# Row scaling of the second layer on VectorE in two halves, and a new order of work inside a step of a two-layer graph attention kernel

## The chip, the cores and the metric

The kernel runs on one core of one Trainium2 chip. The metric is the device time of one execution in microseconds. The core's engines run their own instruction streams and meet through semaphores: TensorE (PE, with weight loads shown as PEld), VectorE (DVE), ScalarE (ACT), GpSimd (POOL) and SyncE (SP).

## The reference

A graph of N = 6250 nodes and E = 200000 edges, sorted by destination, goes through a layer norm, a ReLU and two graph attention (GAT) layers with 256 features, the first with 4 heads, the second with 1. Each edge has 32 attributes. Cut to what matters, one layer is:

```
te  = relu(edge_attr @ We + be) * exp(x @ Wo + bo)[src][:, None]   # 64 per edge
# self loops are added; their attribute is the mean of a node's incoming te
hx  = x @ Wg                                   # 256 per node
he  = te @ Wge                                 # enters the logits through a_e
al  = leaky_relu((hx . a_s)[src] + (hx . a_d)[dst] + he . a_e, 0.2)
m   = segment_max(al, dst)
al  = exp(al - m[dst]);  al = al / segment_sum(al, dst)[dst]
out = segment_sum(hx[src] * al[:, :, None], dst) + b
```

The first layer ends in relu(out + x), the second in out + x; the input is added at the end. Everything is float32.

## The kernel before, in words

**Tiling.** The sorted edges are cut into chunks of 128 and superchunks of C = 24 chunks (3072 edges). A layer has 66 superchunks; each is one *step*, described by a dictionary `st`. The loop `edges` (line 788) runs over the 132 steps of both layers. In the iteration of step `st` the next step `nx` is prepared. The last three steps of each layer are handled by `ending` (line 885), so 63 iterations of each layer take the regular path.

**What a step does**, with the function, the line and the engine:

- `gather` (L1065, POOL): 24 indirect DMAs fetch the rows `hx[src]` and a few columns beside them from a table in HBM, one row per partition and one chunk per DMA, into the tile G (128 x 24 x 270). There are three G buffers. A gather into a buffer waits until the sums of the step that used it before have ended. POOL does hardly anything else, so it runs ahead of the other engines.
- `spread` (L1189, L1190, DVE, once for two steps): builds one-hot tiles of the edges' places within their step, `lb` and Q. `parts` (L1296 to L1299, DVE, once for two steps; L1304, PE) splits the destination logits of the nodes into three bfloat16 parts and brings them into the layout wanted. `blocks` (L1311, DVE) copies them into a block form `aq`. `adst` (L1318, 2 matmuls) adds the destination's part to the logits of the edges.
- `rphase1` (L1165, PE; L1166, ACT): relu of the edge attributes times We, in pieces; `rphase2` (L1174, 8 matmuls): their product with the folded a_e. Both, and `adst`, end in one PSUM tile `zad`.
- `edge_rows` (L1332, L1335, DVE): turns `zad` into logits per edge. `logits` (L1346 to L1363, DVE) adds the source part and runs segmented maximum scans. `ends` (L1370, PE), `links` (L1380, L1382, DVE; L1387, PE) and `maxima` (L1397 to L1423, DVE, with the exp L1419 on ACT) carry the maxima across the partitions' borders and yield the weights exp(al - m). `ends` and `links` use the PSUM tile `lf`.
- scaling: G's rows are multiplied by the weights. In layer 0 `scale` does this for all 24 chunks in one VectorE instruction (L1454, 128 x 6144). In layer 1 `scale_rows` does it in 24 instructions of ScalarE (L1463, 128 x 256 each).
- `carried` (L1436 to L1444, DVE): adds the sum carried over from the step before to G's first row.
- `sums` (L1473, PE): per chunk one float32 product of a one-hot tile S (edge to destination) with G, added up in the PSUM tile `u`. In the trace one chunk is two weight loads and two matmuls, so a step has 48 of each.
- `onehots` (L1280, L1283, DVE): S for the next step. `evict` (L1478, ACT): `u` to SBUF. `finish` and `rows1` to `rows3`: the softmax's division, self loops, node update and, in layer 0, the table rows of layer 1.

**The order** is written out by hand: each engine executes in the order in which the loop body issues. Before the change it is: gather(nx), logits, ends, spread(nx), parts(nx), first piece of rphase1(nx), links, rows2, blocks(nx), maxima, the other pieces of rphase1(nx), rphase2(nx), adst(nx), scaling, carried, sums, rows3, onehots(nx), finish of the step before, evict, rows1, edge_rows(nx). The SP queue only issues loads and stores (`nodes` ahead of the gather, `load_lb`, `load_fl` after rows2, `load_ea` after rphase1) and the DMA instructions of `rows3`.

The one place that chooses between the engines is `st["rows"] = st["L"].l`: it is 0 in layer 0 and 1 in layer 1, and `maxima` and the loop test it.

Of the kernel before, what the change touches and what calls it, by code (L numbers as in the profile page):

```python
# [22 lines left out]
F32 = mybir.dt.float32  # L23
# [8 lines left out]
P = 128  # L32
C = 24
# [48 lines left out]
class Kernel:  # L82
# [705 lines left out]
    def edges(self, ctx):  # L788
        nc = self.nc
        steps = self.steps  # L790
        if self.NS % 2:
            self.load_lb(1)
        pv = late = None
        self.ahead, self.rest = 1, None
        for k, st in enumerate(steps):
            nx = steps[k + 1] if k + 1 < len(steps) else None
            if st["s"] + 2 >= self.NS:
                continue
            for q in steps[k + 1:k + 3]:
                if q["L"] is st["L"] and "tw" not in q:  # L800
                    self.nodes(q)
            self.load_lb(k + 2)
            left = 99
            if self.ahead < len(self.groups):
                left = self.groups[self.ahead][0] - 2 - (self.ahead + 2 >= len(self.groups)) - k
            if self.rest is None and left <= 2:
                gi = self.index_load(self.ahead, self.xp)
                self.rest = self.index_group(self.ahead, self.xp, gi)
            if st["L"].l and (st["s"] == 2 or st["s"] + 3 == self.NS) and not hasattr(self, "flag_i"):
                self.flag()  # L810
                if self.early:
                    self.window()
            if st["s"] + 3 == self.NS:
                self.ending(st, *steps[k + 1:k + 3], pv, late, steps[k + 3] if k + 3 < len(steps) else None)
                pv = late = None
                continue
            if 3 <= k + 1 < 6 and nx["L"].l == 0:
                nx["own"] = steps[k - 2]["G"]
            if k:
                self.gather(nx)  # L820
                st["rows"] = st["L"].l
                drain(self.logits(st))
                self.ends(st)
            self.spread(nx)
            self.parts(nx)
            y = self.rphase1(nx)
            next(y)
            if k:
                self.links(st)
            if late:  # L830
                self.rows2(late)
            self.load_fl(k + 1)
            self.blocks(nx)
            if k:
                drain(self.maxima(st))
            drain(y)
            self.load_ea(k + 2)
            self.rphase2(nx)
            self.adst(nx)
            if "S" not in st:  # L840
                self.onehots(st)
            if k:
                if st["rows"]:
                    self.scale_rows(st)
                else:
                    drain(self.scale(st))
                self.carried(st)
                self.sums(st)
            if late:
                self.rows3(late)  # L850
                late = None
            self.onehots(nx)
            if pv:
                drain(self.finish(pv))
            self.evict(st)
            if pv:
                self.rows1(pv)
                late = pv
            self.index_on(left)
            if k == 4 and self.early:  # L860
# [287 lines left out]
    def rphase1(self, st):  # L1148
# [11 lines left out]
        for a, b in self.pieces(c):  # L1160
# [5 lines left out]
            nc.scalar.activation(R[:, :, w], y[:, :, :n], AF.Relu, bias=self.be[l])  # L1166
            yield

    def rphase2(self, st):

        nc, l, R = self.nc, st["L"].l, st["R"]
        for w, o in self.halves(st):
            for i in range(2):
                nc.tensor.matmul(st["zad"][i * PH:(i + 1) * PH, o], self.wea[l][0], R[:, i, w],  # L1174
                                 start=True, stop=False)
# [107 lines left out]
            nc.vector.tensor_tensor(st["S"][:, c0:c1, :], self.k_iota.unsqueeze(1).to_broadcast(w),  # L1283
                                    self.loc[:, o + c0:o + c1].unsqueeze(2).to_broadcast(w), op=OP.is_equal)

    def parts(self, st):

        L, V = st["L"], self.nc.vector
        H = L.H
        if "a3" not in st:  # L1290
            q = [q for q in self.steps[st["k"]:st["k"] + 2 - st["k"] % 2] if q["L"] is L and "tw" in q]
            n, i = len(q), st["k"] % 4
            ad = self.tw4[:, i:i + n, L.ad:L.ad + H]
            a3 = self.wp.tile([P, 2, 4, 3], BF, name="a3")
            r = self.wp.tile([P, 2, 4], F32, name="a3r")
            V.tensor_copy(a3[:, :n, :H, 0], ad)  # L1296
            V.tensor_sub(r[:, :n, :H], ad, a3[:, :n, :H, 0])
            V.tensor_copy(a3[:, :n, :H, 1], r[:, :n, :H])
            V.tensor_sub(a3[:, :n, :H, 2], r[:, :n, :H], a3[:, :n, :H, 1])  # L1299
            for j, t in enumerate(q):  # L1300
                t["a3"] = a3[:, j]
        a3 = st["a3"]
        st["zad"] = z = self.ps_1.tile([P, 1024], F32, name="zad")
        self.nc.tensor.matmul(z[:, 400:400 + 3 * H], st["Q"], a3[:, :H, :].rearrange("p h t -> p (h t)"),  # L1304
                              start=True, stop=True)
# [159 lines left out]
    def sums(self, st, *parts):  # L1465
        nc, L, c = self.nc, st["L"], st["C"]
        G, S = st["G"], st["S"]
        for a, b in parts or ((0, c),):
            for i in range(a, b):
                j = st["n"] = st.get("n", -1) + 1  # L1470
                if j == 0 and "u" not in st:
                    st["u"] = self.ps_1.tile([P, 512], F32, name="u")
                nc.tensor.matmul(st["u"][:, :L.W], S[:, i, :], G[:, i, 0:L.W], start=(j == 0), stop=(j == c - 1))  # L1473
# [282 lines left out]
def drain(g):  # L1756
    for _ in g:
        pass
# [85 lines left out]
```

## Time and profile before

| | |
|---|---|
| median of 3 runs | 4928.91 us (4916.35 to 4935.57) |
| profiled execution | 4925.46 us |
| its span, first to last instruction | 4923.7 us |
| mean granted TensorE clock | 0.725 |
| regular steps of layer 0 | about 220 to 2374 us |
| regular steps of layer 1 | about 2608 to 4838 us |

The regular steps of the two layers make up 4384 of 4924 us. Within each layer the 63 steps are alike, so a step's time, times 63, is what a change is worth there. In the profile's lines a group shows its instructions (after x), their busy time, the mean of one and the engine's idle time before them with what ended most of it; "issue" means that the engine waited for nothing that the profile shows, and "remote" that the releaser is not known.

### The profile page before, as it was taken

To read this page: it belongs to the slowest core of one execution; us is meant where nothing else is said; L and a number is where in the kernel's file an instruction comes from. 1 tells how busy PE (TensorE), PEld (TensorE's weight loads), DVE (VectorE), ACT (ScalarE), POOL (GpSimd) and SP (SyncE) were. 2 spreads that over 40 slices of the span, in tenths; PEclk is the share of its full clock that TensorE was granted. 3 is DMA by queue.
4 is the path that set the end of the run, shared out by engine and by line. 5 is a ranking of instruction groups with operands and counts; after the bars stand their busy time and mean duration, and the time that the engine had idled before them with its cause. 6 is when DMAs were issued, how large, how long until landed. Compare 5 with 4: busy or idle time off the path is not lost.

```text
span 4923.7 us, 38114 instructions
## 1 busy us (share of the span) xinstructions
PE 2940.4 (60%) x10100; PEld 1841.8 (37%) x10100; DVE 2462.7 (50%) x6148; ACT 1132.2 (23%) x2701; POOL 2989.0 (61%) x3216
## 2 busy tenths in 40 slices
PE   6655666666666666665646556555565555655656
PEld 5433433343333434343434333333333333333334
DVE  5556666676666666666734323333333332333335
ACT  4211111111111111111103323233233332323322
POOL 6356666666666666666544656656666666666663
PEclk8777777777777777777777667667667676666767
DMA  7144444444444444444433434434444443443442
GB/s 223 55 119 125 126 128 134 123 135 132 133 124 128 135 126 131 129 135 122 122 109 92 121 106 115 122 105 119 114 118 114 112 121 107 116 118 107 118 117 71
DMA packets 248253, 591.97 MB, mean 120 GB/s; under 512 B 65849, under 2 KB 105125, under 8 KB 247783
## 3 DMA queue, kind: packets, MB, share of 16 engines
q0 software_dynamic: 150048, 422.51, 32.7%
q1 hardware_dynamic: 97009, 164.82, 10.5%
q10 hardware_dynamic: 976, 2.12, 0.2%
q8 instruction: 86, 1.41, 0.1%
q14 instruction: 134, 1.10, 0.1%
HBM read 544.23 MB, written 45.36 MB: 120 GB/s over the span
## 4 chain that ended last, share of the span: by engine, by line
issue 29%; PE 28%; DVE 21%; POOL 13%; another core or an unknown queue 5%; DMA 3%; ACT 1%; SPq 0%; DVEq 0%; ACTq 0%; POOLq 0%
PE u L1473 21%; POOL G L1065 12%; DVE G L1454 7%; DMA G<-T,src 3%; PE y L1165 2%; DVE S L1283 2%; PE zad L1174 2%; DVE m L1402 1%; DVE lb L1189 1%; DVE rt L1332 1%; ACT R L1166 1%; DVE t1rows L1638 1%; DVE fb L1397 0%; PE lf L1370 0%
## 5 line engine op out<-in xcount | busy, mean ns | idle before, releaser
L1065 POOL DMA_INDIRECT G<-T,src x3066 | 2912.9, 950 | 1824.8 <-issue 949.2
L1473 PE MATMUL u<-G,S 128*128 128x270 f32 (+1 forms) x6212 | 1873.3, 448 | 1419.9 <-issue 1202.2
L1473 PEld LDWEIGHTS u<-G,S 128*128 128x128 f32 x6212 | 1355.8, 221 | 1871.8 <-issue 1438.5
L1463 ACT ACTIVATE G<-G,kw 128x256 f32<-128x256 f32 x1512 | 609.0, 496 | 0.0
L1380 DVE TENSOR_TENSOR_SCAN cl<-fl,cl,lf 4x129 f32<-4x129 f32 (+1 forms) x130 | 61.1, 470 | 1007.6 <-PE zad L1304 940.1
L1478 ACT ACTIVATE U<-u 128x270 f32<-128x270 f32 (+1 forms) x130 | 51.0, 393 | 2169.3 <-PE u L1473 1686.5
L1454 DVE TENSOR_TENSOR G<-G,kps 128x6144 f32<-128x6144 f32 (+6 forms) x86 | 441.7, 5150 | 0.0
L1283 DVE TENSOR_TENSOR S<-kps,loc 128x3072 f32<-128x3072 f32 (+1 forms) x135 | 438.1, 3245 | 4.7
L1165 PE MATMUL y<-ea,webd 64*128 64x256 f32 (+2 forms) x1056 | 355.0, 762 | 41.0 <-ACT R L1166 35.3
L1174 PE MATMUL zad<-R,wea 128*64 128x384 f32 (+1 forms) x1056 | 285.0, 677 | 156.6 <-issue 87.5
L1166 ACT ACTIVATE R<-y,webd 128x1024 f32<-128x1024 f32 (+3 forms) x264 | 235.4, 892 | 427.5 <-PE y L1165 161.9
L1174 PEld LDWEIGHTS zad<-R,wea 128*64 128x64 f32 x1056 | 82.9, 177 | 395.8 <-issue 263.4
L1505 DVE SCALAR_TENSOR_TENSOR mg<-U,mw 128x1 f32<-128x1 f32 x65 | 14.4, 221 | 364.1 <-remote 170.6
L1165 PEld LDWEIGHTS y<-ea,webd 64*128 64x128 f32 x1056 | 116.0, 269 | 105.6 <-issue 59.3
L1332 DVE STREAM_TRANSPOSE rt<-zad 128x768 f32<-128x768 f32 (+1 forms) x130 | 125.8, 968 | 5.4 <-remote 5.4
L567 PE MATMUL fin<-wg,h1T 128*128 128x260 f32 x264 | 116.8, 587 | 1.5 <-ACT h1T L1565 1.5
L1189 DVE TENSOR_TENSOR lb<-lb,kps 128x1536 bf16<-128x1536 bf16 (+1 forms) x68 | 112.9, 1661 | 0.0
L1436 DVE SCALAR_TENSOR_TENSOR G<-U,kw,G 1x257 f32<-1x257 f32 x62 | 29.5, 476 | 152.4 <-issue 87.0
L1575 ACT ACTIVATE t1rows<-t1rows 128x1 f32<-128x1 f32 x66 | 13.4, 203 | 363.9 <-DVE t1rows L571 147.4
L1370 PE MATMUL lf<-ident,fb 128*36 128x128 f32 (+1 forms) x132 | 52.0, 394 | 55.8 <-DVE fb L1363 45.6
L1318 PE MATMUL zad<-lb,aq 128*128 128x384 bf16 (+2 forms) x264 | 83.8, 409 | 0.0
L1515 ACT ACTIVATE mw<-mw 128x8 f32<-128x8 f32 x66 | 13.8, 209 | 298.7 <-issue 146.9
(275 smaller groups left out, 2366.7 us busy)
## 6 DMA issues: line engine op xcount, KB each, us to landing
ea<-in_ea_dram SPq DMA_DIRECT2D x64, 768.0 KB
G<-T,src POOLq DMA_INDIRECT x3066
lb<-locrow SPq DMA_DIRECT2D x64, 384.0 KB
nd<-t1rows SPq DMA_DIRECT2D x66, 225.8 KB
tw<-nd SPq DMA_DIRECT2D x66, 225.8 KB
tw<-T SPq DMA_DIRECT2D x66, 117.2 KB
T<-t1rows SPq DMA_DIRECT2D x66, 113.8 KB
tw<-in_x_dram SPq DMA_DIRECT2D x66, 112.0 KB
```

The source lines that it names most:

```text
L567: self.nc.tensor.matmul(ps[:, :L.MW], hT[:, k, :], self.wg[L.l][:, k, :], start=(k == 0), stop=(k == 1))
L1065: nc.gpsimd.indirect_dma_start(out=G[:, c, 0:L.TW], out_offset=None, in_=st.get("from", self.T[L.l])[0:self.N, :], in_offset=bass.Indirect ...
L1165: nc.tensor.matmul(y[:, i, :n], self.webd[l][r, :], ea[r, w], start=True, stop=True)
L1166: nc.scalar.activation(R[:, :, w], y[:, :, :n], AF.Relu, bias=self.be[l])
L1174: nc.tensor.matmul(st["zad"][i * PH:(i + 1) * PH, o], self.wea[l][0], R[:, i, w], start=True, stop=False)
L1189: V.tensor_tensor(lb[:, :, :n], lb[:, :, :n], self.k_part.unsqueeze(2).to_broadcast([P, i, n]), op=OP.is_equal)
L1283: nc.vector.tensor_tensor(st["S"][:, c0:c1, :], self.k_iota.unsqueeze(1).to_broadcast(w), self.loc[:, o + c0:o + c1].unsqueeze(2).to_broad ...
L1318: self.nc.tensor.matmul(st["zad"][:, o], st["aq"].rearrange("p k j -> p (k j)"), st["lb"][:, w], start=False, stop=True)
L1332: V.transpose(rv[:, :32 * c].rearrange("p (b n) -> p b n", b=2), z.rearrange("p (b n) -> p b n", b=2)[:, :, :16 * c])
L1454: nc.vector.tensor_tensor(v, v, pw[:, c0:c1, :].unsqueeze(3) .to_broadcast([P, c1 - c0, H, L.F]), op=OP.mult)
L1463: self.nc.scalar.activation(v, v, AF.Copy, scale=st["w"][:, c:c + 1])
L1473: nc.tensor.matmul(st["u"][:, :L.W], S[:, i, :], G[:, i, 0:L.W], start=(j == 0), stop=(j == c - 1))
```

## The change

`st["rows"]` is set to 0 in both layers, so that layer 1 takes VectorE's `scale` as well; `scale_rows` and a third order for it remain in the text but are not reached. `scale` now runs in two halves of 12 chunks, with `carried` between them. In every iteration but the first the order is: gather(nx), logits, ends, first piece of rphase1(nx), links, rows2, maxima, the other pieces of rphase1(nx), rphase2(nx), first half of scale, carried, second half, spread(nx), sums of chunks 0 to 13, parts(nx), blocks(nx), sums 14 to 18, adst(nx), sums 19 to 23, rows3, onehots(nx), and then as before. `parts` writes its result no longer into columns 400 on of `zad` but, when given a bank, into columns 240 on of the tile `lf`; `zad` is then allocated by `rphase2` through a new helper. In the first iteration the old order stays, with adst and onehots of the next step moved behind each other. `ending` calls `parts` as before.

```diff
             if k:
                 self.gather(nx)
-                st["rows"] = st["L"].l
+                st["rows"] = 0
                 drain(self.logits(st))
                 self.ends(st)
-            self.spread(nx)
-            self.parts(nx)
+            else:
+                self.spread(nx)
+                self.parts(nx)
             y = self.rphase1(nx)
             next(y)
             if k:
@@
             self.load_fl(k + 1)
-            self.blocks(nx)
             if k:
                 drain(self.maxima(st))
-            drain(y)
-            self.load_ea(k + 2)
-            self.rphase2(nx)
-            self.adst(nx)
+            else:
+                self.blocks(nx)
+            if k and st["rows"]:
+                self.scale_rows(st)
+                drain(y)
+                self.load_ea(k + 2)
+            else:
+                drain(y)
+                self.load_ea(k + 2)
+                self.rphase2(nx)
             if "S" not in st:
                 self.onehots(st)
-            if k:
-                if st["rows"]:
-                    self.scale_rows(st)
-                else:
-                    drain(self.scale(st))
+            if not k:
+                self.adst(nx)
+                self.onehots(nx)
+            elif st["rows"]:
...
+            else:
+                f = self.scale(st, cuts=(0, C // 2, C))
+                next(f)
+                self.carried(st)
+                drain(f)
+                self.spread(nx)
+                self.sums(st, (0, 14))
+                self.parts(nx, self.lf)
+                self.blocks(nx)
+                self.sums(st, (14, 19))
+                self.adst(nx)
+                self.sums(st, (19, C))
+                if late:
+                    self.rows3(late)
+                    late = None
+                self.onehots(nx)
             if late:
                 self.rows3(late)
                 late = None
-            self.onehots(nx)
             if pv:
                 drain(self.finish(pv))
             self.evict(st)
@@
+    def zad(self, st):
+
+        if "zad" not in st:
+            st["zad"] = self.ps_1.tile([P, 1024], F32, name="zad")
+
     def rphase2(self, st):
 
+        self.zad(st)
@@
-    def parts(self, st):
+    def parts(self, st, bank=None):
@@
-        st["zad"] = z = self.ps_1.tile([P, 1024], F32, name="zad")
-        self.nc.tensor.matmul(z[:, 400:400 + 3 * H], st["Q"], a3[:, :H, :].rearrange("p h t -> p (h t)"),
+        if bank is None:
+            self.zad(st)
+        st["ad"] = z = st["zad"][:, 400:400 + 3 * H] if bank is None else bank[:, 240:240 + 3 * H]
+        self.nc.tensor.matmul(z, st["Q"], a3[:, :H, :].rearrange("p h t -> p (h t)"),
                               start=True, stop=True)
@@
     def blocks(self, st):
-                                     st["zad"][:, 400:400 + 3 * H].unsqueeze(1).to_broadcast([P, 4, 3 * H]),
+                                     st["ad"].unsqueeze(1).to_broadcast([P, 4, 3 * H]),
```

More of the change, by code (lines that the diff above doesn't have):

```diff
@@ L832, in edges @@
             self.load_fl(k + 1)
-            self.blocks(nx)
             if k:
                 drain(self.maxima(st))
-            drain(y)
-            self.load_ea(k + 2)
-            self.rphase2(nx)
-            self.adst(nx)
+            else:
[8 more added lines that the diff above has]
+                self.rphase2(nx)
             if "S" not in st:
                 self.onehots(st)
-            if k:
-                if st["rows"]:
-                    self.scale_rows(st)
-                else:
-                    drain(self.scale(st))
-                self.carried(st)
-                self.sums(st)
+            if not k:
+                self.adst(nx)
+                self.onehots(nx)
+            elif st["rows"]:
+                self.carried(st)
+                self.sums(st, (0, C // 3))
+                self.spread(nx)
+                self.parts(nx, self.lf)
+                self.sums(st, (C // 3, C))
+                self.rphase2(nx)
+                self.onehots(nx)
[6 more added lines that the diff above has]
+                drain(f)
+                self.spread(nx)
+                self.sums(st, (0, 14))
+                self.parts(nx, self.lf)
+                self.blocks(nx)
+                self.sums(st, (14, 19))
+                self.adst(nx)
+                self.sums(st, (19, C))
+                if late:
+                    self.rows3(late)
+                    late = None
+                self.onehots(nx)
             if late:
```

## The prediction

> **What bounds the kernel now.** I read the page first: engine shares, the chain, the costliest lines.
>
> ```profile
> PE 2940.4 (60%) x10100; PEld 1841.8 (37%) x10100; DVE 2462.7 (50%) x6148; ACT 1132.2 (23%) x2701; POOL 2989.0 (61%) x3216
> ...
> issue 29%; PE 28%; DVE 21%; POOL 13%; another core or an unknown queue 5%; DMA 3%; ACT 1%; SPq 0%; DVEq 0%; ACTq 0%; POOLq 0%
> ...
> L1065 POOL DMA_INDIRECT G<-T,src x3066 | 2912.9, 950 | 1824.8 <-issue 949.2
> L1473 PE MATMUL u<-G,S 128*128 128x270 f32 (+1 forms) x6212 | 1873.3, 448 | 1419.9 <-issue 1202.2
> ...
> L1463 ACT ACTIVATE G<-G,kw 128x256 f32<-128x256 f32 x1512 | 609.0, 496 | 0.0
> ```
>
> No engine is busy more than 61% of the span, and the largest share of the chain is "issue", time without a recorded cause. POOL is the regular part: one gather takes 0.95 us and the next follows 0.30 us later, so the 24 gathers of a step take 24 x 1.25 = 30 us. What POOL waits for between two such streams is in the waits, cut to the 63 regular steps of each layer: first layer 0, then layer 1.
>
> ```profile
> POOL G L1065 <- PE fin L1563: 217.1, 35, 25.0
> POOL G L1065 <- PE u L1473: 143.3, 28, 9.2
> ```
> ```profile
> POOL G L1065 <- PE zad L1304: 376.5, 58, 8.3
> ```
>
> The rows name what PE did last at that moment; the binding event is the end of the sums (L1473), since a gather writes the buffer that those sums read. Layer 1 waits 376.5/58 = 6.5 us a step. Layer 0, without one long wait of 25.0, (217.1 - 25.0 + 143.3)/62 = 5.4 us. So a step is 30 us of gathers and the stretch until the sums of the oldest buffer have ended. Why they end late is seen in the timeline of one step of layer 1 (start, length, engine, line; in brackets the idle time before it).
>
> ```profile
> 3497.76 0.94 POOL L1065 DMA_INDIRECT G<-T,src  x1 [7.00 <-PE zad L1304]
> ...
> 3500.22 0.25 DVE L1423 COPY G<-kw 128x24 f32<-128x24 f32 x1 [0.18 <-ACT kw L1419]
> ...
> 3502.84 9.67 ACT L1463 ACTIVATE G<-G,kw 128x256 f32<-128x256 f32 x24
> ...
> 3502.99 2.83 PE L1174 MATMUL zad<-R,wea 128*64 128x384 f32 x8 [1.22 <-issue]
> 3503.37 0.48 DVE L1436 SCALAR_TENSOR_TENSOR G<-U,kw,G 1x257 f32<-1x257 f32 x1 [2.90 <-issue]
> ...
> 3503.77 0.20 DVE L1444 SCALAR_TENSOR_TENSOR G<-U,slink,G 1x2 f32<-1x2 f32 x1
> ...
> 3505.76 0.82 PE L1318 MATMUL zad<-lb,aq 128*128 128x384 bf16 x2
> ...
> 3506.37 8.86 PE L1473 MATMUL u<-G,S 128*128 128x261 f32 x37
> ...
> 3517.62 0.52 PE L1473 MATMUL u<-G,S 128*128 128x261 f32 x1 [2.39 <-issue]
> ...
> 3519.03 0.29 PEld L1473 LDWEIGHTS u<-G,S 128*128 128x128 f32 x1 [3.31 <-issue]
> ...
> 3526.59 0.95 POOL L1065 DMA_INDIRECT G<-T,src  x1 [0.30 <-issue]
> ...
> 3531.03 3.05 PE L1473 MATMUL u<-G,S 128*128 128x261 f32 x6 [2.21 <-issue]
> ...
> 3534.11 0.39 ACT L1478 ACTIVATE U<-u 128x261 f32<-128x261 f32 x1 [21.41 <-PE u L1473]
> ...
> 3534.35 0.94 POOL L1065 DMA_INDIRECT G<-T,src  x1 [6.81 <-PE zad L1304]
> ```
>
> The sums begin 8.6 us into the step, and 37 of 48 pass in 8.86 us (0.24 us each). Then a matmul and the next weight load stand 1.4 us apart (3517.62, 3519.03), 2.8 us a pair, with "issue" before each. Only some 4 us after the last gather's start the remaining ones run together again. ScalarE's row scaling (9.67 us, ended at 3512.51) is not what the late sums wait for. Something limits how many instructions pass while POOL streams. The windows count them (busy time and, after x, instructions): from POOL's restart to the first stall, in two steps of layer 1 (rows 1 and 2) and two of layer 0 (rows 4 and 5), and inside a stall (row 3).
>
> ```profile
> core 0: us, PE busy (x) PEld busy (x) DVE busy (x) ACT busy (x) POOL busy (x), PEclk, DMA share, GB/s
> 3461.00:3479.00 18.00, 15.18 (x56) 9.40 (x57) 8.41 (x23) 11.92 (x29) 13.73 (x15) 0.75 0.50 148
> 3497.70:3515.50 17.80, 15.62 (x57) 9.55 (x56) 8.21 (x22) 11.99 (x29) 13.48 (x15) 0.72 0.37 98
> 3515.50:3531.00 15.50, 2.90 (x5) 1.62 (x6) 2.70 (x9) 0.00 (x0) 9.29 (x10) 0.57 0.52 135
> 1478.30:1504.60 26.30, 20.53 (x71) 13.92 (x72) 18.80 (x38) 4.26 (x10) 18.95 (x21) 0.77 0.58 166
> 1514.00:1540.50 26.50, 18.04 (x62) 11.20 (x62) 22.23 (x48) 4.12 (x10) 20.33 (x21) 0.74 0.45 119
> 2607.00:2620.00 13.00, 12.92 (x56) 10.42 (x54) 6.00 (x15) 6.26 (x16) 8.78 (x10) 0.89 0.31 83
> 2620.00:2639.00 19.00, 0.00 (x0) 0.00 (x0) 0.00 (x0) 0.00 (x0) 12.97 (x14) 0.59 0.37 98
> 2639.00:2662.00 23.00, 17.37 (x65) 11.40 (x65) 10.60 (x32) 12.56 (x30) 1.89 (x2) 0.74 0.11 32
> ```
>
> Layer 1 reaches 56+57+23+29+15 = 180 and 57+56+22+29+15 = 179 instructions after 18.0 and 17.8 us; layer 0 reaches 212 and 203 after 26.3 and 26.5. Row by row that is one budget that grows with time, (207 - 180)/(26.4 - 17.9) = 3.2 a us: an estimate from four rows. In the stall, 5 matmuls and 6 weight loads pass in 15.5 us.
>
> The last three rows, from layer 1's first step, tell what follows when the sums do end in time. All 48 ended inside the stream; then in 19 us every engine but POOL executed nothing (x0) while POOL issued 14 gathers, and only after that the engines ran a whole step in 22 us. The timeline of that place:
>
> ```profile
> 2639.62 0.39 ACT L1478 ACTIVATE U<-u 128x261 f32<-128x261 f32 x1 [26.36 <-remote]
> ...
> 2649.24 11.47 PE L1473 MATMUL u<-G,S 128*128 128x261 f32 x48
> ...
> 2660.99 0.94 POOL L1065 DMA_INDIRECT G<-T,src  x1 [20.18 <-PE fin L1049]
> ```
>
> **The change, part by part.** *Row scaling of layer 1.* 24 instructions of ScalarE (496 ns each, L1463) go, and with them PE's wait for each row. VectorE gets two halves; a whole one is in the rows of layer 0:
>
> ```profile
> 1514.08 0.94 POOL L1065 DMA_INDIRECT G<-T,src  x1 [4.82 <-PE u L1473]
> ...
> 1515.70 1.73 DVE L1189 TENSOR_TENSOR lb<-lb,kps 128x1536 bf16<-128x1536 bf16 x1
> ...
> 1517.35 0.42 DVE L1190 TENSOR_TENSOR Q<-kps,qsel 128x256 bf16<-128x256 f32 x1
> 1517.68 0.17 DVE L1296 CAST a<-tw 128x8 bf16<-128x8 f32 x1
> ...
> 1522.20 6.54 DVE L1454 TENSOR_TENSOR G<-G,kps 128x6144 f32<-128x6144 f32 x1
> 1522.98 0.95 POOL L1065 DMA_INDIRECT G<-T,src  x1 [0.30 <-issue]
> ```
>
> So 6.54/2 = 3.3 us a half. The maxima end at 3500.47, 2.7 us into the step; half one ends at 6.0, the carried row (0.48 + 0.20, less a little overlap) at 6.7, half two at 10.0. PE cannot begin sums before its own L1174 group ends (3505.82, 8.1 us), where now 0.8 us of L1318 follows. The sums thus begin at 8.1 instead of 8.6 us: by durations alone the gain is 0.5 us. The half-two wait is covered, since the first 12 chunks are 24 matmuls, 5.8 us at 0.24.
>
> *Spreading, parting, blocks* (1.73 us in every second step, four small casts, one product) leave the head of the step and run on VectorE beside the sums. In layer 0 they stand ahead of the links: in the step above the spreading held VectorE from 1515.70. PE's L1304 and L1318 now stand inside the sums behind chunks 14 and 19. What queues behind them are the last ten and five chunks. VectorE's part is ready at about 10.0 + 1.73 + 0.42 + 0.7 = 12.9 us (1517.35 and 1517.68, the other three casts taken as the first), before PE reaches chunk 14 at 8.1 + 28 x 0.24 = 14.8 us, so I cost them at nothing; without that cover they would cost the 1 to 2 us of a round trip. No DMA is added. SP's loads keep their order, and POOL's gathers still stand first in its queue; what moves is when their wait is met.
>
> *The instruction budget in layer 1.* This decides. From restart to the end of the sums PE issues 69 matmuls (48 + 8 + 8 + 2 + 1 + 1 + 1) and 69 loads; VectorE, counted by the code's order, about 28; ScalarE 5 instead of 29; POOL 15: 186. At 20 us (8.1 + 48 x 0.24 + 0.8 for the two moved groups = 20.4) the budget is 180 + 3.2 x 2.3 = 187. Before, the same end asked for about 22 more, and the sums fell into the stall with 11 to go. After, they end free of it or with a few pairs in it. Up to three pairs at 2.8 us bring the end to 28 us, still inside the 30 us stream. So I take it that POOL finds its buffer free and streams on without a wait.
>
> *What the next stream then does.* The budget is used up and POOL does not pause; I take the freeze of the three windows. Of 60 us of gathers the engines get about the first 20, and after the second stream POOL waits for a whole step: 20.2 us there (the bracket at 2660.99). Per two steps that replaces 2 x 6.5 = 13.0 us: +7.2, that is +3.6 a step, 63 x 3.6 = +227 us. Bounds: the one long wait of layer 0, 25.0 us, gives (25.0 - 13.0)/2 x 63 = +378; if the engines creep on and only 48 sums are left at the end, 11.5 us (the row at 2649.24), it is (11.5 - 13.0)/2 x 63 = -47. I take 20.2, since it is from layer 1 and from the same kind of step.
>
> *Layer 0.* The sums start earlier in the steps with spreading, at about 9 us, but need 150 of PE, some 40 of VectorE, 8 of ScalarE and 17 of POOL = 215 at 22 us, where the budget is 207 - 3.2 x 4.4 = 193. Some ten pairs stay in the stall, so POOL keeps its wait, at the least seen there. That least is about 4.8 us (the restart at 1514.08 had 4.82 before it): 62 x (5.4 - 4.8) = 37, taken as -40. Bounds: -90 if the late steps all become as the early ones; +378 if the sums escape here, too.
>
> *The rest* (the prologue, the two endings, where little but the order of layer 1's scaling changes) I put at 0, between -10 and +10: three of 66 steps a layer, at most about 3 us each.
>
> Sum, against the profiled execution (4925.46 us, span 4923.7): 4925.5 + 227 - 40 = 5112; the median of the runs shown is 3.4 us above that execution, so 5115.
>
> [...] While L1454 reads two operands (1522.20 to 1528.74) a gather takes 0.95 us (1522.98), which is the mean of all 3066. [...]
>
> **Rivals.** *A, faster: the stall still catches the sums of layer 1.* The point is seven or eight instructions: with four or more pairs left at the stall, 4 x 2.8 us carries the end from 20 past 30 us, and POOL waits again. For it: my 186 and 187 are equal within what I can count. Then layer 1 takes layer 0's least, 4.8 instead of 6.5: 63 x 1.7 = -107, with layer 0's -40: 4925.5 - 147 + 3.4 = 4782.
> *B, no freeze.* POOL never waits in layer 1 and the engines keep up: 63 x 6.5 = -410, -40: 4479. Against it: a step has over 200 instructions, and 30 us at 3.2 pass about 96.
> *C, no change.* The stall ends a fixed time behind the last gather whatever was done before, and the tail of pairs, evictions and restart stays 6.5 us; layer 0's 40 us shrink to under 25: about 4915.
> *D, gathers slowed by VectorE.* Half a scaling, 3.3 us, is lost by POOL in each layer-1 step: 63 x 3.3 = +208, less 40: 5097. The gathers of layer 0 speak against it.
>
> **How the numbers follow.** My forecast has 0.55, A 0.27, B 0.05, C 0.08, D 0.02, and 0.03 goes to layer 0 leaving its waits as well (5112 + 378, about 5490). The forecast's own range is 4925.5 - 47 - 90 = 4790 to 4925.5 + 378 - 10 = 5295, most of it above 5000; less the ends, 4980 to 5270. With A's 4782 the range over both signs is 4765 to 5270. Half a per cent, 25 us, is about what the three runs (4916 to 4936) can tell from no change. Faster: A, B and the low end of the forecast, 0.27 + 0.05 + 0.05 = 0.37. Same: C, 0.08. Slower: 0.50 of the forecast, D and the last, 0.55.
>
> **What would show it.** Right: in layer 1 POOL's waits fall to half their number, each near 20 us; windows in which every engine but POOL has x0; evictions (L1478) idle in pairs, one short and one over 20 us; L1473's "issue" idle falls. L1463 shrinks to the last steps of the layer or goes, and L1454 gets two instructions a step in layer 1. In layer 0 the waits stay at 63, near 4.8. Wrong: POOL's waits in layer 1 keep their number (A or C by their length), gathers over 0.95 us beside L1454 (D), or steps of 30 us without waits (B). The weakest step is the count of 186 against 187.

## The result: 8.8% slower, and the profile after

The changed kernel takes 5363.01 us (median of 4 runs, 5357.17 to 5363.5) against 4927.24 us before: ratio 1.0883, 95% interval 1.086 to 1.0906. The forecast was slower, 5115 us, with a range up to 5270; the loss is 436 us, more than twice the +187 forecast. The profiled execution has a span of 5361.7 us, 438.0 more than before.

The page after, in the same parts as before. The functions moved: sums are L1508 now (L1473 before), `scale` L1489, `blocks` L1346 (L1311), `adst` L1353 (L1318), the matmul of `parts` L1339 (L1304), `evict` L1513 (L1478), the gathers L1092 (L1065).

```profile
PE 3046.1 (57%) x10100; PEld 1889.5 (35%) x10100; DVE 2877.7 (54%) x6336; ACT 528.7 (10%) x1189; POOL 2999.9 (56%) x3216
...
DVE 40%; another core or an unknown queue 37%; PE 11%; issue 7%; POOL 2%; DMA 2%; ACT 1%; DVEq 0%; SPq 0%; ACTq 0%
...
L1092 POOL DMA_INDIRECT G<-T,src x3066 | 2924.5, 954 | 2243.4 <-PE u L1508 1201.4
...
L1346 DVE TENSOR_TENSOR aq<-lf,quad 128x12 bf16<-128x12 f32 (+1 forms) x125 | 24.0, 192 | 1957.0 <-remote 1933.4
L1489 DVE TENSOR_TENSOR G<-G,kps 128x3072 f32<-128x3072 f32 (+5 forms) x274 | 870.9, 3183 | 0.0
```

The work is what it was: ScalarE gave up 609 us, VectorE took over 429 us, PE has the same 10100 matmuls. Two things are new. POOL's idle time rose from 1824.8 to 2243.4 us, by 418.6, nearly the whole loss. And `blocks`, an instruction of 0.19 us, has 1957 us of VectorE's idle time before it. The list of waits, longest sums first, has it on top:

```profile
DVE aq L1346 <- remote: 1933.4, 119, 21.2
```

119 waits of 16.2 us, for a releaser that the profile doesn't know. Where the time went by layer is read from POOL's restarts at the first and last regular stream of layer 0 and at the start of layer 1, before and after:

```profile
241.73 0.94 POOL L1065 DMA_INDIRECT G<-T,src  x1 [21.41 <-issue]
```
```profile
2374.07 0.99 POOL L1065 DMA_INDIRECT G<-T,src  x1 [5.59 <-PE u L1473]
```
```profile
239.66 0.94 POOL L1092 DMA_INDIRECT G<-T,src  x1 [16.43 <-issue]
```
```profile
2612.71 0.94 POOL L1092 DMA_INDIRECT G<-T,src  x1 [9.59 <-PE u L1508]
```
```profile
2913.71 0.94 POOL L1092 DMA_INDIRECT G<-T,src  x1 [20.61 <-PE fin L1076]
```

With the restart at 2660.99 shown in the prediction: layer 0 took 2132.3 us and now takes 2373.0, +240.7; the passage between the layers +14.1; layer 1 to the end of the span 2262.7 and now 2448.0, +185.3; the start -2.1. Both layers lost, layer 0 more, although its scaling kept its engine. POOL's waits in the regular steps, first layer 0, then layer 1:

```profile
POOL G L1092 <- PE u L1508: 578.9, 57, 21.7
```
```profile
POOL G L1092 <- PE u L1508: 559.4, 59, 10.2
```

Without the one of 21.7 us layer 0 has (578.9 - 21.7)/56 = 9.9 us a step (5.4 before), layer 1 559.4/59 = 9.5 (6.5 before). POOL waits in every step: there are no pairs of streams with one long wait between them, as I had forecast. One step of layer 1 after, in time order:

```profile
4170.74 0.94 POOL L1092 DMA_INDIRECT G<-T,src  x1 [9.35 <-PE u L1508]
...
4175.66 0.47 DVE L1415 TENSOR_TENSOR_SCAN cl<-fl,cl,lf 1x129 f32<-1x129 f32 x1 [0.51 <-issue]
...
4183.68 7.92 PE L1508 MATMUL u<-G,S 128*128 128x261 f32 x28
...
4191.44 0.17 PE L1339 MATMUL lf<-a,Q 128*128 128x3 bf16 x1
...
4191.46 2.45 PE L1508 MATMUL u<-G,S 128*128 128x261 f32 x10
...
4199.59 0.94 POOL L1092 DMA_INDIRECT G<-T,src  x1 [0.30 <-issue]
4204.84 0.18 DVE L1346 TENSOR_TENSOR aq<-lf,quad 128x12 bf16<-128x12 f32 x1 [19.30 <-remote]
...
4205.07 0.82 PE L1353 MATMUL zad<-lb,aq 128*128 128x384 bf16 x2 [11.16 <-DVE kps L1313]
...
4205.69 4.56 PE L1508 MATMUL u<-G,S 128*128 128x261 f32 x10
...
4210.52 1.10 POOL L1092 DMA_INDIRECT G<-T,src  x1 [9.98 <-PE u L1508]
```

At 4191.44 PE issues the matmul of `parts`, behind chunk 14. VectorE should go on 0.2 us later with `blocks`. It does so at 4204.84, 5.25 us after the start of the last gather. PE has meanwhile run five more chunks and stands at `adst`, which needs `blocks`. Only then come `adst` (0.82 us) and the last ten matmuls (4.56 us), and POOL restarts 5.7 us after the signal. The windows between (columns as in the prediction):

```profile
core 0: us, PE busy (x) PEld busy (x) DVE busy (x) ACT busy (x) POOL busy (x), PEclk, DMA share, GB/s
4170.70:4193.90 23.20, 16.78 (x57) 10.29 (x57) 12.81 (x25) 2.19 (x4) 17.67 (x19) 0.71 0.61 166
4194.00:4204.80 10.80, 0.00 (x0) 0.00 (x0) 0.00 (x0) 0.00 (x0) 5.01 (x6) 0.64 0.30 82
```

In 10.8 us no engine but POOL executes anything. So the stall of the kernel before is still there. It used to meet independent matmuls, which wait for no other engine and of which one passed every 2.1 to 2.9 us (before, 3517.62 to 3531.03); now it meets a chain from PE to VectorE and back to PE, and nothing passes. When all stops, 57 + 57 + 25 + 4 + 19 = 162 instructions have passed since POOL's restart, fewer than the 179 and 180 of the kernel before; when the signal for `blocks` was due, it was 143 (the same count up to 4191.6), and PE ran five more chunks at full pace. So here a signal was late before matmuls slowed down.

A step of layer 0 goes the same way. The matmul of `parts` stands 22.3 us into the stream that began at 1454.27, `blocks` comes 11.9 us later, and POOL restarts 5.7 us after that:

```profile
1476.53 0.17 PE L1339 MATMUL lf<-a,Q 128*128 128x12 bf16 x1
...
1488.44 0.21 DVE L1346 TENSOR_TENSOR aq<-lf,quad 128x48 bf16<-128x48 f32 x1 [15.18 <-remote]
...
1494.16 0.94 POOL L1092 DMA_INDIRECT G<-T,src  x1 [9.73 <-PE u L1508]
```

In layer 1 the first stream that is hit is the one from 2913.71. POOL had stood still before it, and `blocks` of the step before had come at once (2908.67, 0.06 us after the matmul of `parts`). Still the links began 5.9 us into this stream, the sums 14.0 us and the matmul of `parts` 21.7 us (2935.38), and `blocks` came 12.3 us after that. Matmuls that wait for nobody slow down in this stream after 55 + 55 + 34 + 4 + 19 = 167 instructions (counted up to 2937.5).

```profile
2947.83 0.18 DVE L1346 TENSOR_TENSOR aq<-lf,quad 128x12 bf16<-128x12 f32 x1 [18.38 <-remote]
```

### The profile page after: what moved, and what is told of

It reads as the page before. It is cut to its first block, busy times and chain, and to the rows that moved or that the text cites. A ratio compares the mean times of both kernels' runs of the same rounds, so it can differ in the third digit from the quotient of the medians.

```text
span 5361.7 us, 35333 instructions
## 1 busy us (share of the span) xinstructions
PE 3046.1 (57%) x10100; PEld 1889.5 (35%) x10100; DVE 2877.7 (54%) x6336; ACT 528.7 (10%) x1189; POOL 2999.9 (56%) x3216
## 4 chain that ended last, share of the span: by engine, by line
DVE 40%; another core or an unknown queue 37%; PE 11%; issue 7%; POOL 2%; DMA 2%; ACT 1%; DVEq 0%; SPq 0%; ACTq 0%
DVE G L1489 14%; DVE S L1316 6%; PE u L1508 5%; PE y L1192 2%; DVE lb L1222 2%; POOL G L1092 2%; DVE rt L1367 2%; DMA G<-T,src 1%; DVE m L1437 1%; PE ps L567 1%; PE lf L1405 1%; DVE al L1385 1%; DVE al L1383 1%; DVE fb L1432 1%
## 5 line engine op out<-in xcount | busy, mean ns | idle before, releaser
L1092 POOL DMA_INDIRECT G<-T,src x3066 | 2924.5, 954 | 2243.4 <-PE u L1508 1201.4
L1508 PE MATMUL u<-G,S 128*128 128x270 f32 (+1 forms) x6212 | 1864.4, 454 | 404.2 <-issue 371.7
L1508 PEld LDWEIGHTS u<-G,S 128*128 128x128 f32 x6212 | 1377.1, 226 | 920.1 <-issue 609.6
L1346 DVE TENSOR_TENSOR aq<-lf,quad 128x12 bf16<-128x12 f32 (+1 forms) x125 | 24.0, 192 | 1957.0 <-remote 1933.4
L1489 DVE TENSOR_TENSOR G<-G,kps 128x3072 f32<-128x3072 f32 (+5 forms) x274 | 870.9, 3183 | 0.0
L1353 PE MATMUL zad<-lb,aq 128*128 128x384 bf16 (+2 forms) x264 | 103.7, 494 | 742.6 <-DVE kps L1313 711.6
L1316 DVE TENSOR_TENSOR S<-kps,loc 128x3072 f32<-128x3072 f32 (+1 forms) x135 | 438.0, 3245 | 4.8
L1192 PE MATMUL y<-ea,webd 64*128 64x256 f32 (+2 forms) x1056 | 406.5, 866 | 49.1 <-issue 25.4
L1207 PE MATMUL zad<-R,wea 128*64 128x384 f32 (+1 forms) x1056 | 308.0, 725 | 175.6 <-issue 134.5
L1353 PEld LDWEIGHTS <-aq 128*128 128x128 bf16 x264 | 23.8, 119 | 812.0 <-DVE aq L1346 793.1
L1538 ACT ACTIVATE mw<-mw,mg 128x2 f32<-128x2 f32 x66 | 19.7, 298 | 1779.5 <-DVE mg L1537 1779.5
L1598 PE MATMUL fin<-ident,fb 128*128 128x128 f32 x132 | 35.1, 356 | 200.6 <-ACT fb L1587 172.9
L567 PE MATMUL fin<-wg,h1T 128*128 128x260 f32 x264 | 134.5, 663 | 1.5 <-ACT h1T L1600 1.5
L1610 ACT ACTIVATE t1rows<-t1rows 128x1 f32<-128x1 f32 x66 | 13.4, 203 | 1232.7 <-DVE t1rows L571 1222.0
```

The source lines that it names most:

```text
L567: self.nc.tensor.matmul(ps[:, :L.MW], hT[:, k, :], self.wg[L.l][:, k, :], start=(k == 0), stop=(k == 1))
L1092: nc.gpsimd.indirect_dma_start(out=G[:, c, 0:L.TW], out_offset=None, in_=st.get("from", self.T[L.l])[0:self.N, :], in_offset=bass.Indirect ...
L1192: nc.tensor.matmul(y[:, i, :n], self.webd[l][r, :], ea[r, w], start=True, stop=True)
L1353: self.nc.tensor.matmul(st["zad"][:, o], st["aq"].rearrange("p k j -> p (k j)"), st["lb"][:, w], start=False, stop=True)
L1489: nc.vector.tensor_tensor(v, v, pw[:, c0:c1, :].unsqueeze(3) .to_broadcast([P, c1 - c0, H, L.F]), op=OP.mult)
```

## The experiments

The theories were named R (the round trip L1339 - L1346 - L1353 inside the sums is caught by the stall), F (my forecast: sums that end ahead of the stall let POOL stream on, and everything freezes) and S (VectorE has too much to do). Each ratio is against the kernel before on the same chip. The first four ran on a chip where the kernel before took 4863 us, not 4927.

### e1_ahead: the round trip ahead of the sums

```diff
                 drain(f)
                 self.spread(nx)
-                self.sums(st, (0, 14))
                 self.parts(nx, self.lf)
                 self.blocks(nx)
-                self.sums(st, (14, 19))
                 self.adst(nx)
-                self.sums(st, (19, C))
+                self.sums(st)
```

> The changed kernel with parts, blocks and adst of the next step moved ahead of all sums (the second half of the scaling, spread, parts, blocks, adst, then 24 chunks). Theory R (the round trip PE L1339 - VectorE L1346 - PE L1353 inside the sums is caught by the stall, and the last ten matmuls wait behind it): POOL's wait between streams falls from about 9.7 us to 4.8-6.5 a step, 4750 to 4950 us. Theory F (my forecast: sums that end before the stall let POOL stream on and everything freezes): half as many waits of POOL, each near 20 us, about 5100. Theory S (VectorE now has too much to do in a step): no change, 5250 or more.

Measured 4828.9 us, 0.9925 (0.9902 to 0.9947) of the kernel before, from 1.0883 by one move. What VectorE's `blocks` (here L1344) waited for, and POOL's waits in layer 1:

```profile
  issue: 11.5, 45
  PE lf L1337: 4.9, 19
```
```profile
POOL G L1090 <- PE lf L1403: 131.7, 28, 5.1
POOL G L1090 <- remote: 124.0, 28, 4.5
```

`blocks` lost 17 us in the whole kernel instead of 1957, and POOL waits (131.7 + 124.0)/56 = 4.6 us a step in layer 1; in layer 0 it is 301.8/52 = 5.8. R holds, S falls: VectorE has the same work here. F falls, too: POOL's waits did not halve in number.

### e2_behind: only adst moved, behind the sums

```diff
-                self.sums(st, (14, 19))
-                self.adst(nx)
-                self.sums(st, (19, C))
+                self.sums(st, (14, C))
+                self.adst(nx)
```

> The changed kernel with only adst moved, from chunk 19 to behind chunk 23. R: PE no longer waits in the middle of the sums, so they end before the last gather; blocks still holds VectorE until the stall is over, so onehots, finish and the edges' rows come late. POOL's wait falls to about 5 us, 4750 to 5200 us, the range because the late VectorE work can push the next sums into the stall. F: two streams without a wait, then one long one, about 5100. S: no change, 5300 or more.

Measured 5137.11 us, 1.0557 (1.0519 to 1.0594). POOL's waits, layer 0 and layer 1:

```profile
POOL G L1091 <- PE u L1507: 498.5, 54, 11.4
```
```profile
POOL G L1091 <- PE u L1507: 380.1, 58, 8.9
```

Layer 1 gains (6.6 us a step instead of 9.5), layer 0 hardly (9.2 instead of 9.9): I had expected about 5 in both. PE's half of the round trip is thus a part of the loss. The rest I put down to VectorE's half: `blocks` is still held through the stall (1657.8 us of idle time before it, in 116 waits, instead of 1933.4 in 119), and one-hots, finish and edge rows stand behind it, so that the next sums begin late. No run took that half away alone.

### e3_scale: only the scaling of the change, in the old order

```diff
-                st["rows"] = st["L"].l
+                st["rows"] = 0
```

> The kernel before with one change: VectorE scales layer 1's rows, too, whole (one instruction of 6.4 us), in the old order. R: no round trip inside the sums, 24 instructions less a step; the sums start about 1.5 us later in layer 1 and meet a shorter stall: 4820 to 4960 us. F: the sums end ahead of the stall, waits of POOL in layer 1 halve in number: about 5100. S: 3 us more in each step of layer 1: 5110.

Measured 4784.49 us, 0.9827 (0.9803 to 0.9852), less than the 4820 to 4960 that R gave. The scaling alone is a gain, a small one but clear of 1; the order costs. A step of its layer 1:

```profile
4015.08 0.94 POOL L1065 DMA_INDIRECT G<-T,src  x1 [4.55 <-remote]
...
4024.67 13.69 PE L1473 MATMUL u<-G,S 128*128 128x261 f32 x48 [1.77 <-issue]
...
4048.99 0.39 ACT L1478 ACTIVATE U<-u 128x261 f32<-128x261 f32 x1 [19.81 <-PE y L1165]
...
4049.22 0.94 POOL L1065 DMA_INDIRECT G<-T,src  x1 [4.23 <-PE y L1165]
```

This is the case that my forecast turned on, and it came out another way. All 48 matmuls are in the trace by 4038.36, 23 us into the stream and 6.6 us ahead of its end. But the eviction that waits for them starts at 4048.99, and POOL's next stream, which waits for them as well, at 4049.22. POOL did not run past the stall: it waited 4.23 us for the same sums. So a step took 30 us of gathers and some 4.2 us until the signals arrived, 34.2 here. The profile models where matmuls end, so whether they ended late or their signal was late can't be told from it.

### e4_rows: the changed order, ScalarE scaling layer 1

```diff
-                st["rows"] = 0
+                st["rows"] = st["L"].l
```

Layer 1 thereby takes the third order that the diff holds (8 chunks of sums, spread, parts, 16 chunks, rphase2, onehots, blocks, adst).

> The changed kernel with ScalarE scaling layer 1's rows again, through the third order that the diff adds for it (carried, 8 chunks, spread, parts, 16 chunks, rphase2, onehots, blocks, adst); layer 0 keeps the changed order. R: layer 0 stays about 4 us a step slower than before (+250); in layer 1 the round trip stands behind the sums, so its steps are 35 to 39 us: 5100 to 5350. S: layer 1 returns to 36.4 us a step: 5170. F: layer 0 as after, layer 1 as before, 5170.

Measured 5129.89 us, 1.0547 (1.0518 to 1.0576). POOL's waits, layer 0 and layer 1:

```profile
POOL G L1092 <- PE u L1508: 504.4, 53, 11.4
```
```profile
POOL G L1092 <- PE u L1508: 349.5, 57, 7.5
```

Layer 0 keeps its loss (9.5 us a step); layer 1, with the round trip behind the sums, is at 6.1. The three theories gave much the same times here, so this run doesn't tell them apart. What it shows is that the loss of layer 0 doesn't come from layer 1's scaling. It comes from the new order, since the halves of the scaling cost nothing by themselves (e5_halves, below).

### e5 to e8, first on a chip without the stall

Four more kernels were made. On the chip that they met first the kernel before took 4019.24 us, and all but the one with a pause took the same: e5_halves 1.0006 (0.9997 to 1.0015), e6_early 1.0006 (0.9987 to 1.0026), e7_dummy 1.0011 (1.0001 to 1.002), e8_pause 1.2485 (1.2462 to 1.2507). There was no stall in these runs: in the trace of e6_early POOL's longest wait between 400 and 4000 us is 0.3 us. POOL's line on the page of e6_early, the changed kernel with other cuts in its sums, reads

```profile
L1092 POOL DMA_INDIRECT G<-T,src x3066 | 2924.6, 954 | 964.3 <-issue 908.1
```

964 us of idle time instead of 2243, 908 of them the gaps of 0.30 us. A regular step of e6_early is 24 x (0.954 + 0.30) = 30.1 us, POOL's own pace, and the other two kernels without a pause took the same time (4020.21 and 4023.22 us, e6_early 4023.6). The changed kernel itself was not run there. That it would cost nothing is likely from e6_early, which has the same instructions, but not shown. Nor can it be told whether the stall belongs to a chip or to the occasion, since each chip was met once. The four went once more to another chip, where the kernel before took 4859.97 us; those runs tell the theories apart.

### e6_early: the same round trip, ten chunks earlier

```diff
-                self.sums(st, (0, 14))
+                self.sums(st, (0, 4))
                 self.parts(nx, self.lf)
                 self.blocks(nx)
-                self.sums(st, (14, 19))
+                self.sums(st, (4, 8))
                 self.adst(nx)
-                self.sums(st, (19, C))
+                self.sums(st, (8, C))
```

> The changed kernel with the same round trip inside the sums, only earlier: parts and blocks behind chunk 4 (not 14), adst behind chunk 8 (not 19). Theory R (the stall catches the round trip because it stands late): it now ends about 16 us into the stream, before the stall, and the time falls to that of e1_ahead, 0.99 to 1.00 of the kernel before. Rival R2 (any round trip inside the sums costs these microseconds, wherever it stands): 1.05 or more.

> The kernel of e6_early once more (round trip at chunks 4 and 8), since on the chip of that run the kernel before took 4019 us and showed no stall. On a chip with the stall (kernel before at 4800 us or more): theory R (the stall catches the round trip because it stands late) 0.98 to 1.00; rival R2 (a round trip inside the sums costs these microseconds wherever it stands) 1.05 or more. On a chip without the stall 1.00.

Measured with the stall 4779.88 us, 0.9833 (0.9816 to 0.9849). The round trip, 9.4 us into a stream of layer 1 that began at 4008.36, and POOL's waits in layer 1:

```profile
4017.71 0.17 PE L1339 MATMUL lf<-a,Q 128*128 128x3 bf16 x1
...
4017.92 0.18 DVE L1346 TENSOR_TENSOR aq<-lf,quad 128x12 bf16<-128x12 f32 x1
```
```profile
POOL G L1092 <- remote: 243.2, 54, 4.6
POOL G L1092 <- PE y L1192: 18.3, 4, 4.6
```

`blocks` starts at once, and (243.2 + 18.3)/58 = 4.5 us is the floor; layer 0 waits 283.5/49 = 5.8, as in e1_ahead. The kernel has every instruction of the changed one and only other cuts, and by the two ratios it takes 0.9833/1.0883 = 0.904 of its time. This settles what was left open of R: a round trip inside the sums is not what costs, but that it stood so late in the stream. Two things moved with it, though. The signals are no longer held, and VectorE's work behind `blocks` comes early, so that the sums begin 6.9 us into the stream and not 12.9. How much each is worth no run separates.

### e7_dummy: 24 tiny activations more

```diff
-                if st["rows"]:
-                    self.scale_rows(st)
-                else:
-                    drain(self.scale(st))
+                drain(self.scale(st))
+                for _ in range(24):
+                    nc.scalar.activation(self.dum[:, 1:2], self.dum[:, 0:1], AF.Copy)
```

(with e3_scale's edit, and `dum` a new tile of 128 x 2)

> e3_scale with 24 tiny activations a step on ScalarE, on data that nobody reads, where the row scaling stood. ScalarE has nothing else to do there. Theory B (the stall begins when a number of instructions has passed, about 180 at 18 us, as my prediction counted): it begins 6 to 7 us earlier, catches the sums, and layer 1 returns to about 36.5 us a step; 0.995 to 1.02 of the kernel before. Theory T (the stall begins a fixed time into the stream): no change against e3_scale, 0.983.

> The kernel of e7_dummy once more (24 tiny activations a step on the idle ScalarE). On a chip with the stall: theory B (the stall begins when a number of instructions has passed) 0.995 to 1.02 of the kernel before; theory T (a fixed time into the stream) 0.983 as e3_scale. On a chip without the stall 1.00.

Measured with the stall 4878.11 us, 1.0025 (1.0008 to 1.0043), against 0.983 without them (0.9826 for e5_halves on the same chip). A step of layer 1:

```profile
4004.44 10.98 PE L1474 MATMUL u<-G,S 128*128 128x261 f32 x41 [1.02 <-DVE G L1455]
...
4017.14 0.38 PE L1474 MATMUL u<-G,S 128*128 128x261 f32 x1 [1.72 <-issue]
...
4029.64 0.94 POOL L1066 DMA_INDIRECT G<-T,src  x1 [5.31 <-PE zad L1305]
```
```profile
3994.60:4015.40 20.80, 17.92 (x60) 10.81 (x60) 17.17 (x32) 7.26 (x29) 15.88 (x17) 0.68 0.46 119
```

The sums begin as in e3_scale, 9.8 us into the stream, but now 41 matmuls pass, not 48, and then one every 2.1 to 2.8 us (4017.14 to 4026.94). The engine that got the extra instructions had nothing else to do, and nobody waits for them. So here more instructions brought the stall on sooner: 60 + 60 + 32 + 29 + 17 = 198 had passed at its beginning, 20.8 us into the stream, where e3_scale ran 23.5 us without one. The number isn't a fixed one, as the 167 in the changed kernel shows. The size was smaller than expected: 35.0 us a step, not 36.5.

### e8_pause: a pause in the gathers

```diff
+            if j == 20 and last == C - 1 and not own:
+                for _ in range(8):
+                    nc.gpsimd.memset(G[:, 19:23, :], 0.0)
             nc.gpsimd.indirect_dma_start(
```

(with e3_scale's edit; j counts the gathers of a step)

> e3_scale with POOL kept from issuing gathers for about 8 us after the 20th of each 24 (eight memsets of a part of the buffer that the last four gathers then overwrite). If it is POOL's stream that holds back the signals of finished work, they get through in the pause, some 4 us after its start, POOL finds its buffer free at the end of the 24 and waits less than 1 us there: a step of 30 + 8 + 1 = 39 us, 1.07 of the kernel before. If the signals are held for another reason, the wait of 4.3 us stays: 42 us a step, 1.17.

> The kernel of e8_pause once more. There, without the stall, a step took 30 us of gathers and 8 us of memsets, and POOL waited for nothing: 5017 us. On a chip with the stall: if POOL's stream holds back the signals, they get through in the pause and POOL again hardly waits at the end of the 24 gathers: 5020 to 5200 us. If they are held for another reason, the wait of 4.3 us stays: 5550 us.

Measured with the stall 5228.64 us, 1.0754 (1.0733 to 1.0776), a little over the 5200 expected. The timeline around a pause, and its windows:

```profile
4015.37 0.94 POOL L1068 DMA_INDIRECT G<-T,src  x1 [0.30 <-issue]
4016.31 8.42 POOL L1067 MEMSET G<- 128x1080 f32 x8
4020.26 0.39 ACT L1481 ACTIVATE U<-u 128x261 f32<-128x261 f32 x1 [24.06 <-remote]
...
4025.00 0.95 POOL L1068 DMA_INDIRECT G<-T,src  x1 [0.27 <-POOL G L1067]
```
```profile
4005.00:4016.30 11.30, 0.00 (x0) 0.00 (x0) 0.00 (x0) 0.00 (x0) 8.56 (x10) 0.70 0.40 106
4016.30:4020.20 3.90, 0.00 (x0) 0.00 (x0) 0.00 (x0) 0.00 (x0) 3.73 (x5) 0.50 0.13 39
```

During the last ten gathers ahead of the pause nothing else runs. 3.95 us after POOL turns from gathers to memsets, though POOL is as busy as before, the eviction starts that had waited 24.06 us, and the engines run. At the end of the 24 gathers POOL finds its buffer free: in layer 1 it has no wait over 2.3 us, and a step is 30 + 8.4 us. So it is the stream of indirect DMAs that holds the signals here, not POOL being busy, and it took 3.95 us without a new one to end that. Whether it ends because none is issued or because the last ones have landed, the trace doesn't tell.

### e5_halves: scaling in halves, old order

```diff
-                    drain(self.scale(st))
+                    f = self.scale(st, cuts=(0, C // 2, C))
+                    next(f)
                 self.carried(st)
+                if not st["rows"]:
+                    drain(f)
                 self.sums(st)
```

(with e3_scale's edit)

> The kernel before with VectorE scaling both layers in two halves and the carried row between them, all else in the old order (e3_scale, but halves). The runs so far say that a step cannot be shorter than 30 us of gathers and about 4.2 us until POOL sees the end of the sums. Layer 1 stood at 34.3 us a step in e3_scale, so nothing is left there; layer 0 stood at 35.2, and sums that start 3.2 us earlier should bring it to 34.5: e3_scale less 45 us, 0.975 of the kernel before. Rival: layer 0's late steps come from the spreading ahead of the links, not from the scaling, then it equals e3_scale, 0.983.

> The kernel of e5_halves once more. On a chip with the stall: 0.975 of the kernel before if layer 0's late steps come down to 34.5 us, 0.983 if they stay as in e3_scale. On a chip without the stall 1.00.

Measured with the stall 4775.79 us, 0.9826 (0.981 to 0.9842): the rival, no gain beyond e3_scale. A step of layer 1:

```profile
4007.99 10.89 PE L1476 MATMUL u<-G,S 128*128 128x261 f32 x48
...
4034.42 0.39 ACT L1481 ACTIVATE U<-u 128x261 f32<-128x261 f32 x1 [19.66 <-remote]
...
4034.66 0.95 POOL L1068 DMA_INDIRECT G<-T,src  x1 [4.43 <-remote]
```

The sums end 18.4 us into the stream, 5 us earlier than in e3_scale, and what waits for them still starts when the stream is over (4034.42). e3_scale, e5_halves and e6_early beat both kernels where the stall is; against the kernel before it is 1.7%. Where it wasn't, e5_halves and e6_early took the same time as the kernel before; e3_scale was not run there.

## Why the prediction was wrong

- **What bounds the kernel** was read rightly: 30 us of gathers, then a wait until the end of the sums has been seen, with a stall between. The stall comes from the stream (e8_pause) and is brought on by instructions (e7_dummy). The count, 180 at 18 us and 3.2 more a us, is rough. It gives 198 at 23.5 us, where e3_scale had passed 193 without a stall of its matmuls, and 189 at 20.8, where e7_dummy stalled at 198. But in the changed kernel's stream from 2913.71 matmuls already slowed at 167, 23.8 us into it.
- **Spreading, parting, blocks inside the sums**: costed "at nothing", without cover "1 to 2 us of a round trip" (before, from `ends` on PE through `links` on VectorE and back took 1.41 us, 3497.28 to 3498.69). This is the step that failed. The round trip takes 13.4 us (4191.44 to 4204.84), and 5.7 us of PE's work stand behind it when the stream has ended. I placed it at 14.8 us into the stream from durations alone; it stood at 20.7, since the sums began 12.9 us into the step, not at 8.1. The 8.1 rested on links that begin with POOL's restart, as in the old order (3497.74 and 3497.76). In the new order `blocks` stands only some 5 us of PE's work ahead of the end of the sums, while one-hots, finish and edge rows, 9.9 us of VectorE, stand behind it (4165.73 to 4175.66); so the links began 4.9 us after the restart. The order alone does that, without the stall: the stream from 2913.71 had its links at 5.9 us although `blocks` had come at once, and it was the first to be hit.
- **What the next stream does**: forecast, half as many waits of POOL of 20 us each. Measured, a wait in each step, 9.5 and 9.9 us. The freeze of all engines that I took from layer 1's first step is real (10.8 us in the step from 4170.74 after). That POOL passes the end of its stream was wrong: it waits for the same held-back signal (4.23 us in e3_scale, 4.43 in e5_halves). The +227 for layer 1 (+185 measured) was thus near by another mechanism, and that the kernel became slower, as forecast, was luck.
- **Layer 0**: forecast -40, measured +240.7. The instruction count said rightly that the sums would fall into the stall there, but I took the wait to stay at its least; the round trip ahead of the last ten matmuls was not in that count (11.9 us to `blocks` and 5.7 behind it, in the step from 1454.27). This term is the largest part of the miss: with it alone put right 5112 would be 5112 + 281 = 5393, for 5363.5 measured.
- **Row scaling of layer 1**: worth about 0.5 us a step by durations, which said nothing of the instructions saved. Alone it gains 1.7% (e3_scale): layer 1's wait falls to some 4.4 us ((166.6 + 81.9)/57), close to the 4.8 of rival A, but not by A's mechanism, since by the trace no sums are left in the stall there (48 matmuls by 4038.36) and only what waits for them is late (4048.99). A had 2.9% (4782 of 4927).
- **Rivals**: A failed for the change as a whole. B (no freeze, POOL's own pace) is what the chip without the stall shows for the orders tried there. C and D are out. D's sign would have been slow gathers: their mean is 954 ns, before 950 (in layer 1 alone 951 and 948), with 6.5 us of scaling now in every step.

What the stall is made of stays open: no run here shows what holds the signals back, only that it ended 3.95 us into the pause of e8_pause while POOL worked on.

## What to carry to other kernels

The round trip from PE to VectorE took 13.4 us here, where its two instructions took 0.17 and 0.18: durations said nothing of the late signal. Look in the trace at which point of a step signals arrive late, and keep every round trip ahead of that point (0.9833 in e6_early, 1.0883 as it stood) or make it independent of what ends the step. When work is moved under another engine's work, ask not only whether that cover is long enough, but what stands behind the moved piece on both engines: here ten matmuls on one, and on the other 9.9 us of work that the next step needs first. When one change holds two edits, try each alone: here one was worth 1.7%, and both together cost 8.8%.

## What the runs showed of the hardware

- While POOL issued indirect DMAs one after another (0.95 us each, 0.30 between), the other engines were held after 167 to 212 instructions (167 in the changed kernel, 179 and 180 in layer 1 before, 198 in e7_dummy, 203 and 212 in layer 0 before): independent matmuls passed one in 2.1 to 2.9 us (before, 3517.62 to 3531.03; e7_dummy, 4017.14 to 4026.94), and work that waited for PE's results started only about 4 us after the end of the last gather (3.95 us in e8_pause, 4.0 in e3_scale, 4.3 in the changed kernel). POOL being busy with memsets did not hold them: in e8_pause the engines ran again 3.95 us into 8.42 us of memsets.
- It was not there on every chip: the same kernel before took 4927, 4863 and 4860 us in three sets of runs and 4019 us in a fourth, on another chip, where POOL's gathers alone set the pace in e6_early, 30.1 us a step, and e5_halves and e7_dummy took the same time within 0.1%.
- Extra instructions on an idle engine, 24 of about 0.2 us, cost 2% of the time under the stall (4878 us, and 4776 for e5_halves on the same chip) and at most 0.1% without it (1.0011 and 1.0006).
